# Filling two PSUM banks in turns, chunk by chunk, in a macaron layer (FFN, S4D convolution, FFN)

## The chip, the cores and the metric

One core of one Trainium2 chip runs the whole program. The metric is the device time of one execution in microseconds (us). Three runs of the kernel before gave 1369.08, 1369.99 and 1370.74 us; their median, 1369.99 us, is the time before. About 0.2% (2.7 us) is what a measurement of this kernel can tell from no change.

## What is computed

The input x has shape (4, 1024, 256), fp32. Three residual steps follow each other:

```
x = x + 0.5 * ffn(layernorm(x))
x = x + attn(layernorm(x))        # S4D: a causal convolution along the 1024 positions
x = x + 0.5 * ffn(layernorm(x))   # the same weights again

ffn:  h = silu(x @ w1.T * s1) * (x @ w2.T * s2)     # 256 -> 1024, two branches
      h = gelu(h @ h1.T * s3)                        # 1024 -> 1024
      h = gelu(h @ h2.T * s4)                        # 1024 -> 1024
      y = h @ w3.T * s5                              # 1024 -> 256
attn: y = irfft(rfft(x) * rfft(K))[:1024];  gelu(y) @ W.T + b
      K is computed from log_dt, A and C by exponentials, sines and cosines
```

The FFN weights hold only -1, 0 and 1; the scales s are separate vectors.

## The kernel before

**Blocks.** The 4096 tokens are cut into eight blocks of 512, "f0" to "f7" for the first FFN and "g0" to "g7" for the second. Activations lie transposed: 128 channels on the partitions, 512 tokens along the free side, so that 1024 channels are eight chunks of 128x512. f0 to f7, g0 and g1 are done one at a time by `ffn` (L374). The last six blocks are done as three pairs by `ffn_pair` (L416), whose two wide layers are Winograd products of quarters (L510) that the change leaves alone.

**Two parts.** An fp32 activation chunk is held as a rounded fp32r part and the rest: ScalarE (ACT) makes the first by a cast (L389, L401), VectorE (DVE) the second by a subtraction (`low_part`, L309). A weight tile is therefore multiplied twice, with the high part and with the low part. One output tile of a wide layer takes 8 chunks x 2 parts = 16 matmuls of 128x128 by 512 columns into one PSUM bank, one of the first layer 2 x 2 = 4, one of the last layer 16. `linear` (L362) issues them for one bank: all chunks in order, high then low.

**A block.** The first layer makes eight pairs of tiles `pa`, `pb` (eight chunks `ha`): Silu on ACT (L384), the product on DVE (L385), cast, low part. The second and third layer make eight tiles each (`p2` into chunks `h2`, `p3` into `h3`; the trace writes both as `p`): Gelu on ACT (L399), cast (L401), low part (L309). The last layer, `last_squares` (L603), makes two tiles `po` from the eight chunks `h3` with `w3` (L617), scales them on ACT (L628), transposes them on DVE (L629), adds the residual and stores. The last block of all ends in `last_tokens` (L636), which has the tokens on the partitions and is not changed.

So each layer needs all eight chunks of the layer before, and the last chunk comes out latest: Gelu, cast and subtraction still lie between the last matmul of one layer and the last inputs of the next.

**What else runs meanwhile.** After each tile of a wide layer `ffn` calls `ahead()` (the next block's norm and loading, `prepare` L1189) and `tick()` (L1245). A tick lets a generator called `aside` go on until it has spent an allowance of work (`STEP_WORK`, counted from DVE elements): first the convolution kernel (`kernel_steps` L833, with the exponentials of L820 and the sines and cosines of L740 and L741 on ACT, tile names `e_b`, `a_b`, `k_b`, `qd`, `p`, `po` on DVE, and products `pk` on TensorE at L883), later the convolution itself (`mix` L1036; transforms `pf`, `pi` and products `pw` on TensorE, `y` and `z` on DVE). When that pauses, weight sums and a check of the weights (`given`, `sign`) fill in. Work tiles come from a pool of 19 buffers ("half"), the chunks from one of 15 ("ring"), PSUM tiles from one of all 8 banks.

**The order.** The program is written in this order, but a scheduler then places the instructions of every engine, by its own estimate of when inputs and buffers are ready, and that order is fixed in the built program: each engine goes through its list in order, and waits where an input is late. The scheduler may already mix matmuls of two tiles where it expects a chunk late. Different functions on ACT (Gelu, Silu, square root, exponential, sine) need a table load where they alternate.

Of the kernel before, what the change touches and what calls it, by code (L numbers as in the profile page):

```python
# [18 lines left out]
P = 128  # L19
# [89 lines left out]
def macaron_layers(  # L109
# [24 lines left out]
    nc = tc.nc  # L134
    split = bad is not None
    wide = F32R if split else F32
    parts = 2 if split else 1
# [26 lines left out]
    def bank(name):  # L164
        return psum.tile([P, 512], F32, tag="ps", name=name)

    def half(name, *shape, dtype=F32):

        return work.tile([P, *(shape or (512,))], dtype, tag="half", name=name, bufs=19)

    def ring(name, *shape, dtype=F32):

        return work.tile([P, *shape], dtype, tag="ring", name=name, bufs=15)
# [7 lines left out]
    w1_sb = keep.tile([P, DC, HID], wide, name="w1_sb")  # L181
    w2_sb = keep.tile([P, DC, HID], wide, name="w2_sb")
# [124 lines left out]
    def low_part(t, src):  # L307

        return nc.vector.tensor_tensor(t[:, 1, :], src, t[:, 0, :].bitcast(F32), ALU.subtract)  # L309
# [49 lines left out]
            xt.append(t)  # L359
        return xt  # L360

    def linear(ps, w, m, acts):  # L362
        n = len(acts)
        for k in range(n):
            for part in range(parts):
                nc.tensor.matmul(  # L366
                    ps,
                    w[:, k, m * P : (m + 1) * P],
                    acts[k][:, part, :],
                    start=(k == 0 and part == 0),  # L370
                    stop=(k == n - 1 and part == parts - 1),
                )

    def ffn(xt, src, dst, blk, name, tick, ahead, final):  # L374


        ha = []
        for m in range(KH):
            pa, pb = bank(f"pa_{name}_{m}"), bank(f"pb_{name}_{m}")
            linear(pa, w1_sb, m, xt)  # L380
            linear(pb, w2_sb, m, xt)
            g = half(f"g_{name}_{m}")
            t = ring(f"ha_{name}_{m}", parts, TB, dtype=wide)
            nc.scalar.activation(g, pa, AF.Silu, scale=sc_sb[:, 0, m : m + 1])  # L384
            nc.vector.scalar_tensor_tensor(  # L385
                g if split else t[:, 0, :], pb, sc_sb[:, 1, m : m + 1], g, ALU.mult, ALU.mult
            )
            if split:
                nc.scalar.copy(t[:, 0, :], g)  # L389
                low_part(t, g)  # L390
            ha.append(t)
        for layer, w in ((2, h1_sb), (3, h2_sb)):
            hb = []
            for m in range(KH):
                ps = bank(f"p{layer}_{name}_{m}")
                linear(ps, w, m, ha)
                t = ring(f"h{layer}_{name}_{m}", parts, TB, dtype=wide)
                g = half(f"g{layer}_{name}_{m}") if split else t[:, 0, :]
                nc.scalar.activation(g, ps, AF.Gelu, scale=sc_sb[:, layer, m : m + 1])  # L399
                if split:  # L400
                    nc.scalar.copy(t[:, 0, :], g)  # L401
                    low_part(t, g)
                hb.append(t)
                ahead()
                if layer == 2 or m < KH - 1:
                    tick()
            ha = hb
        ahead(last=True)
        if name == "f0":
            nc.scalar.mul(w3s_half, w3s_half, 0.5)  # L410
        if final:
            last_tokens(ha, src, dst, blk, name)
        else:
            last_squares(ha, src, dst, blk, name)()

    def ffn_pair(xts, src, dst, blks, names, tick, ahead, final):  # L416

        pair_name = names[0]
        raw = raw_tiles(f"g_{pair_name}")
        for n, (xt, name) in enumerate(zip(xts, names)):  # L420
            for m in range(KH):
                pa, pb = bank(f"pa_{name}_{m}"), bank(f"pb_{name}_{m}")
                linear(pa, w1_sb, m, xt)
                linear(pb, w2_sb, m, xt)
                g = raw[m // QK, n][m % QK]
                nc.scalar.activation(g, pa, AF.Silu, scale=sc_sb[:, 0, m : m + 1])
                nc.vector.scalar_tensor_tensor(
                    g, pb, sc_sb[:, 1, m : m + 1], g, ALU.mult, ALU.mult
                )
            if n == 0:  # L430
                b11 = operand(raw[0, 0], f"b112_{pair_name}")
        calls = 0

        def step():
            nonlocal calls
            calls += 1
            if calls % 2 == 0:
                ahead()
                if calls < 2 * 7 * QK:
                    tick()  # L440

        raw, b11, _ = winograd(raw, b11, 2, pair_name, step)
        raw, c22, c12 = winograd(raw, b11, 3, pair_name, step)
        c11 = operand(raw[0, 0], f"hl00_{pair_name}")
        end_1 = last_squares(c12 + c22, src, dst, blks[1], names[1], QK)
        c21 = operand(raw[1, 0], f"hl10_{pair_name}")
        ahead(last=True)
        if final:
            end_1(nc.vector, nc.sync)
            last_tokens(c11 + c21, src, dst, blks[0], names[0])  # L450
        else:
            end_0 = last_squares(c11 + c21, src, dst, blks[0], names[0])
            end_1()
            end_0()


    def raw_tiles(name):


        return {  # L460
            (k, n): [
                late.tile([P, TB], F32, tag="raw", name=f"{name}_{k}{n}_{c}", bufs=4 * QK)
                for c in range(QK)
            ]
            for k, n in ((0, 0), (1, 1), (0, 1), (1, 0))
        }

    def operand(quarter, name):

        ops = []  # L470
        for c, src in enumerate(quarter):
            t = ring(f"{name}_{c}", parts, TB, dtype=wide)
            nc.scalar.copy(t[:, 0, :], src)
            low_part(t, src)
            ops.append(t)
        return ops
# [126 lines left out]
    def last_squares(acts, src, dst, blk, name, first=0):  # L603


        rest = []
        for k in range(DC):
            xr = half(f"xr_{name}_{k}", TB // SQ, SQ)
            for c in range(P // SQ):
                nc.sync.dma_start(xr[c * SQ : (c + 1) * SQ], in_squares(src, blk, k, c))  # L610
            rest.append(xr)
        banks = [bank(f"po_{name}_{k}") for k in range(DC)]
        order = [(first + k) % KH for k in range(KH)]
        for o, ps in enumerate(banks):
            for k in order:
                for part in range(parts):
                    nc.tensor.matmul(  # L617
                        ps,
                        w3_sb[:, k, o * P : (o + 1) * P],
                        acts[k][:, part, :],  # L620
                        start=(k == order[0] and part == 0),
                        stop=(k == order[-1] and part == parts - 1),
                    )

        def end(add_on=nc.gpsimd, queue=stores):
            for k, ps in enumerate(banks):
                o, y = half(f"o_{name}_{k}"), half(f"y_{name}_{k}", TB // SQ, SQ)
                nc.scalar.activation(o, ps, AF.Identity, scale=w3s_half[:, k : k + 1])  # L628
                nc.vector.transpose(y, o.rearrange("p (n s) -> p n s", s=SQ))  # L629
                add_on.tensor_tensor(y, rest[k], y, ALU.add)  # L630
                for c in range(P // SQ):
                    queue.dma_start(in_squares(dst, blk, k, c), y[c * SQ : (c + 1) * SQ])

        return end
# [610 lines left out]
    def tick():  # L1245


        nonlocal ticks, allowed, work_done
        ticks += 1
        allowed = min(allowed, work_done) + (  # L1250
            STEP_WORK_2 if ("f", n_blocks - 1) in done else STEP_WORK
        )
        while work_done < allowed:
            at = work_done
            if next(aside, PAUSE) is PAUSE:
                for _ in range(2):
                    if len(done) > 8 and allowed - work_done > OP_WORK + TB:
                        next(fillers, None)
                break
            if work_done == at:  # L1260
                work_done += MIN_WORK
# [7 lines left out]
    xt, last_split = transposed(x_first, "f0")  # L1269
    allowed = work_done  # L1270
    operands = [xt]
    for n, unit in enumerate(units):
# [6 lines left out]
        def ahead(last=False):  # L1279
            if last:  # L1280
                done.extend(("last layer", *b[::-1]) for b in upcoming)
            for step in steps:
                next(step, None)
# [102 lines left out]
```

## Time and profile before

| what | value |
|---|---|
| runs before | 1369.08, 1369.99, 1370.74 us |
| profiled execution, its own time | 1368.44 us |
| its span, first to last instruction | 1366.6 us |
| granted TensorE clock, mean | 0.998 |
| DVE busy | 1010.7 us (74%), 1889 instructions |
| ACT busy | 776.5 us (57%), 1236 instructions |
| POOL busy | 287.9 us (21%) |
| DMA moved | 159.99 MB, mean 117 GB/s |
| L366 matmuls, p_f from ha_f / from h_f | 1024 / 1024 instructions, 238.7 / 237.1 us |
| L617 matmuls, po_f | 256 instructions, 60.7 us |

A row of groups names line, engine, operation, output and inputs by the program's tile names without their numbers (p_f<-ha_f,h_sb is a tile of the second layer of some block of the first FFN), shape, count, busy time and mean duration. "PE" is the matmul side of TensorE, "PEld" its weight loads, "SP" the queue that issues most loads. In a timeline each row is a start, a length (both in us), the engine, the line and the instructions merged into it, and in brackets the idle time of the engine just before, with what ended it. The ends of matmuls are modelled: a pipelined matmul shows as some 390 ns though the next one starts sooner, so rows of matmuls overlap and starts are what counts.

### The profile page before, as it was taken

How to read it: one execution, taken by the hardware profiler on the slowest of the kernel's cores; microseconds unless marked ns; L12 is line 12 of the kernel's file. 1: busy time of each engine (PE TensorE's matmuls, PEld its weight loads, DVE VectorE, ACT ScalarE, POOL GpSimd, SP SyncE). 2: the span in 40 equal slices, each digit the busy share in tenths (PEclk: the TensorE clock that was granted, in tenths of full speed). 3: DMA queues.
4: the chain of work that ended last, by engine and by line, in shares of the span. 5: the costliest groups of instructions: out<-in, count | busy, mean ns of one | idle time of the engine just before them, and what ended most of it. 6: DMA issues, size and time to landing. Idle time of an engine off the chain costs nothing.

```text
span 1366.6 us, 18200 instructions
## 1 busy us (share of the span) xinstructions
PE 1351.7 (99%) x6300; PEld 1124.7 (82%) x6300; DVE 1010.7 (74%) x1889; ACT 776.5 (57%) x1236; POOL 287.9 (21%) x443
## 2 busy tenths in 40 slices
PE   8999999999999999999999999999999999999997
PEld 7888878888888888888888887888888888888886
DVE  6997885749965887668855799658885778568654
ACT  5985966454444543534545745436776576656663
POOL 4440220421205213420114012052300430040000
PEclk9999999999999999999999999999999999999999
DMA  9440121413125235354054352352655145521441
GB/s 357 109 142 5 31 62 39 143 36 123 40 93 199 64 108 190 122 183 123 23 168 116 112 154 47 116 168 79 212 160 168 31 141 179 173 64 62 162 131 49
DMA packets 125637, 159.99 MB, mean 117 GB/s; under 512 B 77968, under 2 KB 88208, under 8 KB 120160
## 3 DMA queue, kind: packets, MB, share of 16 engines
q1 hardware_dynamic: 103520, 99.94, 24.2%
q0 software_dynamic: 21744, 58.55, 13.6%
q8 instruction: 51, 0.84, 0.2%
q14 instruction: 50, 0.41, 0.1%
q10 hardware_dynamic: 272, 0.26, 0.1%
HBM read 120.95 MB, written 37.75 MB: 116 GB/s over the span
## 4 chain that ended last, share of the span: by engine, by line
PE 49%; DVE 4%; DMA 0%; issue 0%; ACT 0%; SPq 0%; DVEq 0%
PE p_g L366 7%; PE p2a_g L510 6%; PE p3a_g L510 6%; PE p3x_g L510 5%; PE p2x_g L510 5%; PE p_f L366 4%; PE pa_g L366 4%; PE pb_g L366 4%; PE po_g L617 3%; PE pi L1134 1%; PE pw L1159 1%; DVE y L155 1%; PE po_f L617 1%; PE pa_f L366 1%; PE pb_f L366 1%; PE pf_m L956 1%
## 5 line engine op out<-in xcount | busy, mean ns | idle before, releaser
L366 PE MATMUL p_f<-ha_f,h_sb 128*128 128x512 f32 x1024 | 238.7, 392 | 0.1
L366 PE MATMUL p_f<-h_f,h_sb 128*128 128x512 f32 x1024 | 237.1, 391 | 0.0
L366 PEld LDWEIGHTS p_f<-h_f,h_sb 128*128 128x128 f32 x1024 | 192.1, 188 | 39.7
L366 PEld LDWEIGHTS p_f<-ha_f,h_sb 128*128 128x128 f32 x1024 | 191.4, 188 | 40.4 <-DVE ha_f L309 0.8
L399 ACT ACTIVATE g_f<-p_f,sc_sb 128x512 f32<-128x512 f32 x128 | 87.4, 689 | 210.6 <-PE p_f L366 183.0
L309 DVE TENSOR_TENSOR h_f<-g_f,h_f 128x512 fp32r<-128x512 f32 x128 | 87.9, 689 | 112.8 <-ACT h_f L401 112.5
L401 ACT CAST h_f<-g_f 128x512 fp32r<-128x512 f32 x128 | 78.4, 619 | 3.1
L524 ACT ACTIVATE h_g<-h_g,sc_sb 128x512 f32<-128x512 f32 x72 | 52.0, 723 | 43.8 <-DVE h_g L480 43.6
L339 POOL DMA_DIRECT2D moved<-sq_f x56 | 30.6, 554 | 198.3 <-DVE sq_f L155 198.3
L366 PE MATMUL pa_f<-xt_f,w_sb 128*128 128x512 f32 x256 | 70.5, 391 | 1.3 <-DVE xt_f L321 0.7
L339 POOL DMA_DIRECT2D moved<-sq_g x64 | 34.9, 552 | 167.1 <-DVE sq_g L155 165.9
L366 PE MATMUL pb_f<-xt_f,w_sb 128*128 128x512 f32 x256 | 69.9, 389 | 0.0
L366 PE MATMUL pa_g<-xt_g,w_sb 128*128 128x512 f32 x256 | 68.9, 389 | 0.0
L366 PE MATMUL pb_g<-xt_g,w_sb 128*128 128x512 f32 x256 | 68.9, 389 | 0.0
L617 PE MATMUL po_f<-h_f,w_sb 128*128 128x512 f32 x256 | 60.7, 391 | 1.6 <-ACT h_f L401 0.9
L385 DVE SCALAR_TENSOR_TENSOR g_f<-pb_f,sc_sb,g_f 128x512 f32<-128x512 f32 x64 | 46.6, 745 | 20.2 <-ACT g_f L384 10.5
L366 PE MATMUL p_g<-ha_g,h_sb 128*128 128x512 f32 x256 | 59.4, 391 | 0.1
L366 PE MATMUL p_g<-h_g,h_sb 128*128 128x512 f32 x256 | 59.3, 391 | 0.0
L630 POOL TENSOR_TENSOR y_g<-xr_g,y_g 128x512 f32<-128x512 f32 x12 | 17.0, 1424 | 197.5 <-DVE y_g L629 183.8
L617 PEld LDWEIGHTS po_f<-h_f,w_sb 128*128 128x128 f32 x256 | 47.6, 188 | 13.0 <-DVE h_f L309 2.0
L366 PEld LDWEIGHTS pa_f<-xt_f,w_sb 128*128 128x128 f32 x256 | 48.0, 188 | 12.2 <-DVE xt_f L356 1.0
L399 ACT ACTIVATE g_g<-p_g,sc_sb 128x512 f32<-128x512 f32 x32 | 22.1, 689 | 60.8 <-PE p_g L366 49.5
(302 smaller groups left out, 2879.9 us busy)
## 6 DMA issues: line engine op xcount, KB each, us to landing
w<-q SPq DMA_DIRECT2D x42, 1024.0 KB, 5.0
q<-s POOLq DMA_DIRECT2D x40, 256.0 KB, 4.3
h_sb<-in_h_dram POOLq DMA_DIRECT2D x8, 1024.0 KB, 14.2
given<-in_h_dram SPq DMA_DIRECT2D x32, 256.0 KB, 3.4
kr<-k_hat SPq DMA_DIRECT2D x20, 256.0 KB, 2.7
ki<-k_hat SPq DMA_DIRECT2D x20, 256.0 KB, 3.0
q<-h_sb POOLq DMA_DIRECT2D x16, 256.0 KB, 4.4
xr_f<-in_x_dram SPq DMA_DIRECT2D x64, 64.0 KB, 2.5
```

The source lines that it names most:

```text
L155: return op(dst, *args, **kwargs)
L309: return nc.vector.tensor_tensor(t[:, 1, :], src, t[:, 0, :].bitcast(F32), ALU.subtract)
L339: stores.dma_start(moved[k].rearrange("(c r) a q -> a r c q", r=SQ)[a], sq[a * SQ : (a + 1) * SQ].rearrange("r c j s -> r c (j s)"),)
L366: nc.tensor.matmul(ps, w[:, k, m * P : (m + 1) * P], acts[k][:, part, :], start=(k == 0 and part == 0), stop=(k == n - 1 and part == parts ...
L385: nc.vector.scalar_tensor_tensor(g if split else t[:, 0, :], pb, sc_sb[:, 1, m : m + 1], g, ALU.mult, ALU.mult)
L399: nc.scalar.activation(g, ps, AF.Gelu, scale=sc_sb[:, layer, m : m + 1])
L401: nc.scalar.copy(t[:, 0, :], g)
L510: nc.tensor.matmul(ps, weights[:, c, m * P : (m + 1) * P], ops[c][:, part, :], start=(first and c == 0 and part == 0), stop=(c == QK - 1 a ...
L524: nc.scalar.activation(o, src, AF.Gelu, scale=sc_sb[:, layer, m : m + 1])
L617: nc.tensor.matmul(ps, w3_sb[:, k, o * P : (o + 1) * P], acts[k][:, part, :], start=(k == order[0] and part == 0), stop=(k == order[-1] an ...
L630: add_on.tensor_tensor(y, rest[k], y, ALU.add)
L956: nc.tensor.matmul(ps[e][:, part, :], m[:, e, part, :], rows_of(q + JQ * e), start=True, stop=True)
```

## The change

`linear` takes several (bank, weights, tile) at once and goes through the chunks on the outside, through the banks inside. Three callers use it with two banks: the two branches of the first layer (`pa` and `pb`, in `ffn` and `ffn_pair`), the first two tiles of each of the two wide layers in `ffn`, and, by its own loops, the last layer's two banks in `last_squares`. The number of matmuls, their operands and every other instruction that is written stay the same; only the order is written differently. In the wide layers both banks of the first two tiles are now taken before the first tile's Gelu, `ahead()` and `tick()`.

```diff
-    def linear(ps, w, m, acts):
+    def linear(outs, acts):
         n = len(acts)
         for k in range(n):
-            for part in range(parts):
-                nc.tensor.matmul(
-                    ps,
...
+            for ps, w, m in outs:
+                for part in range(parts):
+                    nc.tensor.matmul(
+                        ps,
+                        w[:, k, m * P : (m + 1) * P],
+                        acts[k][:, part, :],
+                        start=(k == 0 and part == 0),
+                        stop=(k == n - 1 and part == parts - 1),
+                    )
...
-            linear(pa, w1_sb, m, xt)
-            linear(pb, w2_sb, m, xt)
+            linear([(pa, w1_sb, m), (pb, w2_sb, m)], xt)
...
             hb = []
+            first = [bank(f"p{layer}_{name}_{m}") for m in range(2)]
+            linear([(ps, w, m) for m, ps in enumerate(first)], ha)
             for m in range(KH):
-                ps = bank(f"p{layer}_{name}_{m}")
-                linear(ps, w, m, ha)
+                if m < 2:
+                    ps = first[m]
+                else:
+                    ps = bank(f"p{layer}_{name}_{m}")
+                    linear([(ps, w, m)], ha)
...
-        for o, ps in enumerate(banks):
-            for k in order:
+        for k in order:
+            for o, ps in enumerate(banks):
                 for part in range(parts):
```

More of the change, by code (lines that the diff above doesn't have):

```diff
@@ L360, in parted @@
         return xt
-    def linear(ps, w, m, acts):
+    def linear(outs, acts):
         n = len(acts)
         for k in range(n):
-            for part in range(parts):
-                nc.tensor.matmul(
-                    ps,
[L368 to L372, printed above, removed]
+            for ps, w, m in outs:
[7 more added lines that the diff above has]
+                    )
     def ffn(xt, src, dst, blk, name, tick, ahead, final):
@@ L422, in ffn_pair @@
                 pa, pb = bank(f"pa_{name}_{m}"), bank(f"pb_{name}_{m}")
-                linear(pa, w1_sb, m, xt)
-                linear(pb, w2_sb, m, xt)
+                linear([(pa, w1_sb, m), (pb, w2_sb, m)], xt)
                 g = raw[m // QK, n][m % QK]
```

## The prediction

> **What bounds the kernel now.** I read the page's engine rows first, then who TensorE waits for, then the chain in order of time, then the stages with waits.
>
> ```profile
> span 1366.6 us, 18200 instructions
> PE 1351.7 (99%) x6300; PEld 1124.7 (82%) x6300; DVE 1010.7 (74%) x1889; ACT 776.5 (57%) x1236; POOL 287.9 (21%) x443
> ```
> ```profile
> PE po_f L617 <- ACT h_f L401: 0.9, 1, 0.9
> PE po_f L617 <- DVE h_f L309: 0.7, 1, 0.7
> PE po_g L617 <- DVE h_g L309: 0.6, 1, 0.6
> PE po_g L617 <- ACT h_g L401: 0.3, 1, 0.3
> ```
> ```profile
> 1096.98 7.25 PE p2a_g L510 x32
> ```
>
> TensorE (PE) is busy 99%, but its ends are modelled, so I go by starts: 32 wide matmuls in 7.25 us (third fence) is 227 ns each, and 5408 of them make 1226 us. All that PE waits for is listed in eight rows, 6.6 us together, of which 2.6 are the very first. Counting late starts instead of named waits, with the slow start after each pause, I find about 6 us in the body: 2.2 at f1's last layer (the po rows), 1.5 at g0's last layer, 0.9 at f6's, 0.4 at f0's, and 0.5 and 0.4 at the second layer of f1 and g1. The change can take away no more than these 6 us.
>
> Why so few: the scheduler already mixes banks where it expects a late chunk.
>
> ```profile
> 171.72 6.51 PE L617 MATMUL po_f<-h_f,w_sb 128*128 128x512 f32 x28
> 172.18 1.28 ACT L740 ACT_TABLE_LOAD   x1
> 173.47 0.63 ACT L740 ACTIVATE a_b<-a_b 128x512 f32<-128x512 f32 x1
> 174.01 0.71 ACT L741 ACTIVATE k_b<-k_b,cst_sb 128x512 f32<-128x512 f32 x1
> 176.43 1.28 ACT L399 ACT_TABLE_LOAD   x1 [1.71 <-DVE k_b L155]
> 177.73 0.69 ACT L399 ACTIVATE g_f<-p_f,sc_sb 128x512 f32<-128x512 f32 x1
> 178.44 0.62 ACT L401 CAST h_f<-g_f 128x512 fp32r<-128x512 f32 x1
> 179.12 0.73 PE L617 MATMUL po_f<-h_f,w_sb 128*128 128x512 f32 x2 [0.89 <-ACT h_f L401]
> 179.82 0.69 DVE L309 TENSOR_TENSOR h_f<-g_f,h_f 128x512 fp32r<-128x512 f32 x1
> 180.57 0.30 PEld L617 LDWEIGHTS po_f<-h_f,w_sb 128*128 128x128 f32 x2 [1.16 <-DVE h_f L309]
> ```
>
> At f1's last layer PE did 28 matmuls first: all seven ready chunks of *both* banks. The order that the change writes was in place, and PE still stood, because ACT put a sine/cosine with two table loads before the eighth tile's Gelu. What ends last here is the queue on ACT and DVE. The stages say the same:
>
> ```profile
> 36.00:90.00 54.00, 54.00 (x238) 44.24 (x237) 52.66 (x127) 49.87 (x68) 21.01 (x39) 1.00 0.46 140
> 792.00:830.00 38.00, 37.13 (x163) 29.95 (x162) 37.75 (x84) 16.09 (x23) 3.29 (x6) 1.00 0.47 131
> ```
> (start:end and length, then busy PE, PEld, DVE, ACT, POOL.) In f0's second half DVE is busy 52.7 of 54 us and ACT 49.9; in g0's last part DVE 37.75 of 38. There a chunk's time is set by what stands ahead of it on DVE and ACT.
>
> **The change part by part.** The built order of the changed kernel can be read without running it. Matmuls, DVE, POOL and DMA instructions are the same in number; ACT gets 7 more table loads. For each chunk I summed the DVE work ahead of its low part, by the durations in this trace, in both orders. They differ in two places only: f0, and g0's third and last layer. Elsewhere the last chunk stands as before, and its first use comes 14 matmuls later (28 instead of 14, +3.2 us).
>
> *First layer, pa and pb in turns.* The silu starts 2 matmuls (0.45 us) later for each pair of tiles; a pair takes 8 x 227 ns = 1.8 us, ACT needs 1.3 of it and DVE 1.35, and the chunk is needed 6.4 us later. Cost nothing; without the later first use of the chunk it would be 0.45 us a block.
>
> *Second and third layer, first two tiles in turns.* Takes away the 0.5 us at f1 and the 0.4 at g1: -0.9. Nothing else waits there, so the other 18 such boundaries give nothing. The two banks are taken 3.6 us earlier; eight tiles pa/pb held them and were read by then, so no bank wait.
>
> *pk blocks.* The longer head makes the scheduler cut five blocks of 16 pk products (f1 and f2) in two halves with 8 wide matmuls between.
>
> ```profile
> 111.64 0.61 PE L366 MATMUL p_f<-ha_f,h_sb 128*128 128x512 f32 x2
> 112.19 2.05 PE L883 MATMUL pk<-qd,p 128*64 128x32 f32 x32
> ```
> Around this block, single starts go 318 ns into it, and after it one of 335 instead of 227; with what lies between, a change to pk and back costs about 0.3 us. Five more: +1.5 (0.7 to 1.5, if only the change in counts).
>
> *Last layer, f0.* In the changed order DVE has the norm of block f3 and of f2, the products a_b, k_b and four qd ahead of f0's last low part: 7.1 us more than before, against a use that comes 3.2 us later. Why they moved: f0's first two tiles of layer two end together at 31.4 us, DVE idles some 2.5 us for them, and the kernel steps slide to later tiles. ACT: f0's third layer ends its first two tiles at 64.5 us instead of 60.5 (50 matmuls from 53.14 are ahead of that). From the first Gelu there to the last cast, before took 24.6 us (60.59 to 85.16), 0.7 of it waiting. The new list adds two table loads (2.6) and a sine and a cosine (1.3): 27.8 us, so the last high part is there at 92.3. PE starts this layer at 82.15 as before:
>
> ```profile
> 82.15 7.80 PE L617 MATMUL po_f<-h_f,w_sb 128*128 128x512 f32 x32
> ```
> and is done with 28 at 88.5. It then waits to 92.3, fills in with six matmuls of f1, and waits for the low part, by DVE at 94.3 to 96.6. Its 38 matmuls end at 94.7 to 97.1 instead of 90.8: a stall of 3.9 to 6.3, less the 0.4 of before. Value +4.7 (3.5 to 6): both queues are full, so a gain is excluded.
>
> [...]
>
> *Last layer, g0.* From 792.5 DVE has one idle gap of 0.25 us to 830. The changed order has the norm of g4 before the last two chunks: 3.4 us more ahead of the seventh low part, 3.1 ahead of the eighth. They come at 826.9 and 830.5; PE, from 819.29, needs the seventh at 825.2, then stands behind one g1 matmul that needs a copy which DVE makes at 829.5. It ends 35 matmuls at 831.1 instead of 827.2: 3.9 lost instead of 1.5. Value +2.4 (1 to 3.5).
>
> *Last layer, the others.* f1 and f6 have the same order on PE, ACT and DVE around the stall as before, and f1's begins with ACT work that PE itself released at 139 us: they stay, 0 (f6 could lose its 0.9). In the pairs the last layer has no gap: 0.
>
> *Banks in turns as such.* In the trace of before, a start after a change of bank comes 227.8 ns after the last (426 cases), without one 227.1. Some 750 more changes: +0.5, taken as +0.2. [...] Two tiles in turns end together, so nothing of the second covers the first's reading. [...] Only at the end of the program could it show: there the outputs' first half is read 3.6 us later, with DVE done at about 1354.4 and its next input there at 1354.7. Zero.
>
> **Sum**, on the profiled execution (1368.44 us, 1.8 over its span of 1366.6; the median of the runs is 1.55 higher): -0.9 + 1.5 + 4.7 + 2.4 + 0.2 = +7.9, from ends +4 to +12. I shade it to +7.5 for what f6 may give back: 1375.9 for a profiled execution, 1377.5 for the median.
>
> **The rivals.**
>
> *The shifts are swallowed, about no change* (18%): +1, 1371. If DVE or ACT reach f0's eighth chunk by 90.7 us, when PE needs it, f0 loses nothing; likewise g0 by 826.8. For it: the scheduler chose this order by its own estimate, with fillers only for six matmuls. Against: the busy rows above.
>
> *Faster* (7%): 1367. One mechanism: the moved norms and products stand in f0 and g0, where the late first use gives 3.2 us. If ACT's chain in f0 is shorter by over 4 us than my sum, the stalls of f0 and g0 (1.9) go as well as 0.9 in layer two and f6's 0.9, which pays for the pk changes at 0.7: -3.0. It decides at 88.5 us, the end of the 28 matmuls. Against it, ACT alone has 27.8 us of work from 64.5.
>
> *Banks in turns cost TensorE* (10%): 1386. At the program's start single matmuls in turns are 231 to 236 ns apart. If alternation does this, 2144 matmuls by 4 ns are +8.6 on top. Against: 227.8.
>
> **The numbers.** Forecast 65%: 1377.5, own range 1373 to 1382. Faster by over 0.2% (below 1367.2) 7%; within 0.2% 17%, mostly the second case; slower 76%. The range 1370.5 to 1384 takes in the swallowed case's upper part and both ends of the sum, and leaves out the faster case and most of the third.
>
> **What would show it.** Right: PE standing 4 to 6 us between 86 and 97 us and 3 to 4 between 823 and 831, waiting for ACT h_f and DVE h_f, h_g; f1's 2.2 us still there, later; no gap at layer two of f1 and g1; 13 blocks of pk; 227 ns between starts. Wrong: f0's last layer without a stall over 1 us, starts 231 ns apart, or waits of PE in the pairs or for banks.

## The result and the profile after

| kernel | median | runs | ratio to before (95%) |
|---|---|---|---|
| before, same chip | 1369.08 us | 5, 1367.78 to 1370.74 | |
| changed | 1377.52 us | 5, 1376.88 to 1377.67 | 1.0059 (1.0045 to 1.0074) |

The change costs 8.4 us. Its profiled execution took 1377.12 us and has a span of 1375.3 us, 8.7 more than before. First the page's head, then what TensorE (PE) waits for (engine, line, who was waited for: us in all, times, longest).

```profile
span 1375.3 us, 18182 instructions
...
PE 1355.8 (99%) x6300; PEld 1127.2 (82%) x6300; DVE 1012.8 (74%) x1889; ACT 781.3 (57%) x1243; POOL 287.9 (21%) x443
```
```profile
PE po_f L624 <- ACT h_f L408: 3.7, 3, 2.6
...
PE pa_g L369 <- DVE xt_g L356: 1.9, 1, 1.9
PE pa_f L369 <- DVE xt_f L356: 1.5, 1, 1.5
PE po_f L624 <- DVE h_f L309: 1.5, 2, 0.8
```

PE's share is 99% as before, and its busy time has even grown by 4.1 us: the page's first rows would not show where the time went. The waits do: po_f waited for ACT 0.9 us before and 3.7 now, and pa_g's 1.9 us is new. The timelines of those places show how they come about. PE in f0's last layer (start, length, instructions, and in brackets the idle time before and what ended it):

```profile
81.80 4.70 PE L624 MATMUL po_f<-h_f,w_sb 128*128 128x512 f32 x20
86.81 0.73 PE L624 MATMUL po_f<-h_f,w_sb 128*128 128x512 f32 x2 [0.31 <-ACT h_f L408]
88.33 1.65 PE L624 MATMUL po_f<-h_f,w_sb 128*128 128x512 f32 x6 [0.78 <-DVE h_f L309]
92.54 1.22 PE L624 MATMUL po_f<-h_f,w_sb 128*128 128x512 f32 x2 [2.57 <-ACT h_f L408]
93.56 0.63 PE L369 MATMUL pa_f<-xt_f,w_sb 128*128 128x512 f32 x1
...
95.83 0.63 PE L624 MATMUL po_f<-h_f,w_sb 128*128 128x512 f32 x2
```

PE did 28 matmuls by 90.0, stood for 2.57 us, put six matmuls of f1 in between, and did the last two at 95.83. Before, these 32 ran from 82.15 without a pause. What ACT and DVE did meanwhile, first in the changed kernel, then ACT before:

```profile
87.30 1.28 ACT L747 ACT_TABLE_LOAD   x1
88.59 0.63 ACT L747 ACTIVATE a_b<-a_b 128x512 f32<-128x512 f32 x1
89.13 0.71 ACT L748 ACTIVATE k_b<-k_b,cst_sb 128x512 f32<-128x512 f32 x1
...
89.85 1.28 ACT L406 ACT_TABLE_LOAD   x1
91.15 0.69 ACT L406 ACTIVATE g_f<-p_f,sc_sb 128x512 f32<-128x512 f32 x1
...
91.87 0.62 ACT L408 CAST h_f<-g_f 128x512 fp32r<-128x512 f32 x1
...
93.07 1.71 DVE L155 TENSOR_TENSOR qd<-k_b,a_b 64x256 f32<-64x256 f32 x4
94.81 0.69 DVE L309 TENSOR_TENSOR h_f<-g_f,h_f 128x512 fp32r<-128x512 f32 x1
```
```profile
84.56 0.60 ACT L401 CAST h_f<-g_f 128x512 fp32r<-128x512 f32 x1
...
86.48 0.63 ACT L740 ACTIVATE a_b<-a_b 128x512 f32<-128x512 f32 x1
```

A sine, a cosine and two table loads now stand ahead of the eighth Gelu; before, they came after its cast. On DVE four products `qd` stand ahead of its low part, which is there at 95.5. In g0's last layer PE waits for the seventh low part, and then behind a matmul of g1 whose copy DVE makes late, after the norm of another block (`x_g`). First g0 before, then changed:

```profile
826.16 0.73 PE L617 MATMUL po_g<-h_g,w_sb 128*128 128x512 f32 x2 [0.29 <-ACT h_g L401]
827.47 0.73 PE L617 MATMUL po_g<-h_g,w_sb 128*128 128x512 f32 x2 [0.58 <-DVE h_g L309]
```
```profile
833.84 0.73 PE L624 MATMUL po_g<-h_g,w_sb 128*128 128x512 f32 x2 [0.71 <-DVE h_g L309]
836.47 0.80 PE L369 MATMUL pa_g<-xt_g,w_sb 128*128 128x512 f32 x1 [1.90 <-DVE xt_g L356]
```
```profile
835.03 1.05 DVE L155 TENSOR_SCALAR x_g<-x_g,mv_g,rstd_g 128x256 f32<-128x256 f32 x3
836.00 0.75 DVE L356 CAST xt_g<-xf_g 128x512 fp32r<-128x512 f32 x2
```

The stages (start:end, length, busy PE, PEld, DVE, ACT, POOL, then PE's granted clock, DMA share, GB/s); g0's is taken 7 us later than before, since PE is 7 us later there:

```profile
36.00:90.00 54.00, 52.88 (x231) 42.83 (x229) 52.37 (x138) 51.31 (x68) 21.33 (x39) 1.00 0.46 140
799.00:837.00 38.00, 34.98 (x151) 28.09 (x150) 37.95 (x90) 20.06 (x27) 3.31 (x6) 0.99 0.42 128
...
82.00:100.00 18.00, 14.34 (x55) 10.71 (x54) 16.70 (x34) 14.06 (x18) 1.83 (x2) 0.91 0.19 29
```

DVE is as full as before in f0's second half, and ACT is fuller (51.3 of 54 instead of 49.9); in g0's last part DVE is full again (37.95 of 38). In the last row the granted clock is 0.91: after the pause, starts are 427 ns apart instead of 227, until 95.27. That is a cost which the prediction had not. f1's stall is where it was, 28 matmuls and then two waits (0.82 and 0.72 us; before 0.89 and 0.72):

```profile
177.38 6.51 PE L624 MATMUL po_f<-h_f,w_sb 128*128 128x512 f32 x28
184.72 0.73 PE L624 MATMUL po_f<-h_f,w_sb 128*128 128x512 f32 x2 [0.82 <-ACT h_f L408]
...
```

The pk blocks are cut as foreseen (13 instead of 8; three cuts in f1, two in f2), and 32 matmuls of a pair take as long as before:

```profile
116.80 1.12 PE L890 MATMUL pk<-qd,p 128*64 128x32 f32 x16
117.85 2.11 PE L369 MATMUL p_f<-ha_f,h_sb 128*128 128x512 f32 x8
...
```
```profile
1107.29 7.42 PE L516 MATMUL p2a_g<-b_g,w 128*128 128x512 f32 x32
```

(31 starts 227 ns apart and one length of 0.39 are 7.42.) To see where the time goes in all, I set the start of each matmul against the matmul at the same place in PE's list before. The difference is the lag, and a step is what the lag changes by over a stretch. The lag grows by 5.5 us over f0's last layer and f1's first tiles, 0.5 at f1's second layer, 0.7 at f2's, 0.9 at f6's last layer and 3.8 over g0's last and g1's first; it falls by 0.4 at the start and 0.4 at g1's second layer, and does not change in the pairs. At the last matmul it is 10.5 us. The end of the program takes 1.75 back.

### The profile page after: what moved, and what is told of

It reads as the page before. It is cut to its first block, busy times and chain, and to the rows that moved or that the text cites. A ratio compares the mean times of both kernels' runs of the same rounds, so it can differ in the third digit from the quotient of the medians.

```text
span 1375.3 us, 18182 instructions
## 1 busy us (share of the span) xinstructions
PE 1355.8 (99%) x6300; PEld 1127.2 (82%) x6300; DVE 1012.8 (74%) x1889; ACT 781.3 (57%) x1243; POOL 287.9 (21%) x443
## 4 chain that ended last, share of the span: by engine, by line
PE 85%; DVE 6%; ACT 4%; DMA 3%; issue 1%; POOL 0%; SPq 0%; DVEq 0%; ACTq 0%; POOLq 0%
PE p_f L369 26%; PE p_g L369 6%; PE p3a_g L516 6%; PE p2a_g L516 6%; PE p2x_g L516 5%; PE p3x_g L516 5%; PE pa_g L369 4%; PE pb_g L369 4%; PE pa_f L369 4%; PE pb_f L369 4%; PE po_g L624 3%; PE po_f L624 3%; PE pi L1141 2%; PE pf_m L963 2%; PE pw L1166 2%; DMA h_sb<-in_h_dram 2%
## 5 line engine op out<-in xcount | busy, mean ns | idle before, releaser
L369 PE MATMUL pa_f<-xt_f,w_sb 128*128 128x512 f32 x256 | 81.6, 393 | 2.2 <-DVE xt_f L356 1.5
L369 PE MATMUL pa_g<-xt_g,w_sb 128*128 128x512 f32 x256 | 79.8, 392 | 1.9 <-DVE xt_g L356 1.9
L369 PE MATMUL pb_f<-xt_f,w_sb 128*128 128x512 f32 x256 | 81.0, 391 | 0.0
L369 PE MATMUL pb_g<-xt_g,w_sb 128*128 128x512 f32 x256 | 79.2, 390 | 0.0
L406 ACT ACT_TABLE_LOAD x40 | 51.3, 1283 | 27.1 <-PE p_f L369 18.7
L369 PEld LDWEIGHTS pa_g<-xt_g,w_sb 128*128 128x128 f32 x256 | 48.4, 189 | 12.4 <-DVE xt_g L356 2.3
L309 DVE TENSOR_TENSOR ha_f<-g_f,ha_f 128x512 fp32r<-128x512 f32 x64 | 51.8, 832 | 8.6 <-ACT ha_f L391 8.0
```

The lines of the kernel that those rows point to most:

```text
L369: nc.tensor.matmul(ps, w[:, k, m * P : (m + 1) * P], acts[k][:, part, :], start=(k == 0 and part == 0), stop=(k == n - 1 and part == parts ...
```

## Experiments

**Theory A**: the wide layers' tiles in turns make the scheduler build another order in f0 and g0, in which side work stands ahead of the last chunks on ACT and DVE; PE waits for that. **Theory B**: the last layer in turns is the loss. **Theory C**: changes of bank cost PE some ns. The first three runs take the change apart by its three callers, the fourth by its blocks.

| run | what it is | median | before there | ratio (95%) |
|---|---|---|---|---|
| e1_last | last layer alone | 1367.29 | 1368.85 | 0.9992 (0.9985 to 0.9998) |
| e2_wide | wide layers alone | 1379.95 | 1368.85 | 1.0079 (1.0065 to 1.0093) |
| e3_first | first layer alone | 1368.86 | 1368.85 | 1.0000 (0.9992 to 1.0009) |
| e4_not_f0_g0 | all but f0's and g0's wide layers | 1368.43 | 1368.85 | 0.9997 (0.9989 to 1.0005) |
| e5_second_off | all but f0's, g0's second layer | 1372.29 | 1368.58 | 1.0029 (1.0018 to 1.0040) |
| e6_third_off | all but f0's, g0's third layer | 1374.36 | 1368.58 | 1.0040 (1.0027 to 1.0054) |
| e7_filled | changed, pauses filled | 1377.70 | 1368.58 | 1.0067 (1.0053 to 1.0080) |
| e8_end_alone | before, residual loads first | 1367.11 | 1368.58 | 0.9988 (0.9982 to 0.9995) |
| e9_dve_more | e1 with 21 additions more on DVE | 1372.64 | 1368.54 | 1.0031 (1.0020 to 1.0041) |
| e10_fewer_steps | e1 with less side work in f1, g0 | 1366.62 | 1368.54 | 0.9982 (0.9975 to 0.9989) |
| e11_fewer_steps_old | before with less side work | 1367.42 | 1368.54 | 0.9990 (0.9984 to 0.9997) |
| e12_end_and_steps | e8 and e11 together | 1365.44 | 1368.84 | 0.9976 (0.9967 to 0.9985) |

### Each caller alone

Only the last layer:

```diff
-            linear([(pa, w1_sb, m), (pb, w2_sb, m)], xt)
+            linear([(pa, w1_sb, m)], xt)
+            linear([(pb, w2_sb, m)], xt)
...
-            first = [bank(f"p{layer}_{name}_{m}") for m in range(2)]
+            turns = 2 if False else 0
+            first = [bank(f"p{layer}_{name}_{m}") for m in range(turns)]
...
-                if m < 2:
+                if m < turns:
```

> The change cut down to its last layer: the two output banks in turns, first and wide layers as before. The built order leaves ACT's and DVE's work in f0 and g0 as it was, pk in 8 blocks, 92 table loads; SP issues the two residual loads of g6 ahead of the stores of g7, as in the changed kernel. Theory A (the loss is made by the wide tiles in turns of f0 and g0, which move work on ACT and DVE ahead of the last chunks; the last layer in turns is innocent): no loss; f0's 0.4 us and a part of g0's 1.5 go, f1's 2.2 stay, the end of the program is 1.7 shorter: -1.5 to -3.5, so 1365.5 to 1367.5. Theory B (the last layer in turns makes the loss: both banks end late together, nothing is left to do under the last chunk): most of the +8.4, so 1374 to 1378. Theory C (a change of bank costs TensorE some ns): 480 of 2144 matmuls, 4 ns each, +2, less the 1.7 of the end: 1369.5.

Measured 1367.29. Theory B is out. f0's last layer is 0.4 us shorter, of which f1's first tiles give 0.3 back; g0's and f1's steps are 0.0: 28 matmuls under the last chunk instead of 14 gave almost nothing. At the last matmul PE is 0.2 us ahead; the rest of the 1.6 us gained lies behind it.

Only the wide layers (the first and the last layer as before):

```diff
-        for k in order:
-            for o, ps in enumerate(banks):
+        for o, ps in enumerate(banks):
+            for k in order:
```

> The change cut down to the first two tiles of the wide layers; first and last layer as before. The built order has 99 table loads and 13 pk blocks as in the changed kernel, the same 10 table loads in f0's third layer and the same 8 more DVE instructions there. Theory A: all of the loss and none of the gain at the end of the program: +9.5 to +12, so 1378.5 to 1381, with the same waits for h_f and h_g as in the changed kernel. Theory B: about no loss, 1368 to 1370.5. Theory C: 640 of 2144 matmuls, +2.6: 1371.5.

Measured 1379.95, +11.1: all of the loss. Its waits are those of the changed kernel to 0.1 us (po_f for ACT 3.6, pa_g for DVE 1.9).

Only the first layer (the wide and the last layers by the two edits above):

> The change cut down to the first layer: two branches in turns; wide and last layers as before. Same waits and the same order of SP as before. Theory A: nothing, 1369 +- 0.7 (the changed kernel's first layer of f0 starts 0.35 us sooner). Theory B: nothing. Theory C: 1024 of 2144 matmuls by 4 ns, +4: 1373.

Measured no difference. Theory C is out: 1024 of the matmuls in turns cost nothing. The starts say so too: with the banks taken from the built order, and starts over 280 ns left out, those of 128x512 in the changed kernel are 226.9 ns apart after a change of bank (1354 cases) and 226.8 without one (3950).

All of the change, but not the wide layers of f0 and g0:

```diff
+            turns = 2 if name not in ("f0", "g0") else 0
...
```

> The whole change but for the wide layers of f0 and g0, whose tiles come one after the other as before. The built order has 94 table loads, 13 pk blocks, and in f0's and g0's third layer the list of ACT and DVE as before. Theory A: the losses of f0 (5.5) and g0 (3.8) go, the pk cuts (+1.7), f6's 0.9 and the gain at the end (-1.7) stay: 1377.5 - 9.3 = 1368, 1366.5 to 1369.5. Theory B: as the changed kernel, 1376 to 1378. Theory C: 128 matmuls fewer in turns of 2144, so 1377.

Measured 1368.43: without two blocks of sixteen the change costs nothing that can be told. The lag shows what is hidden in this zero: +0.5 at f1's second layer, +0.7 at f2's, +1.1 at f6's last layer, -0.4 at g1's second, and -1.7 at the end.

### Which layer of f0 and g0

```diff
+            turns = 2 if not (layer == 2 and name in ("f0", "g0")) else 0
...
```

> The whole change, but in f0 and g0 the second layer's first two tiles come one after the other as before; their third layer stays in turns. In the built order f0's third layer has the list of ACT and DVE work of before (8 table loads, 43 other DVE instructions), g0's that of the changed kernel. Theory A1 (f0 loses because the second layer's two tiles end together and ACT's and DVE's other work slides behind the third layer's tiles): f0's 5.5 us go, g0's 3.8 stay, 1377.5 - 5.5 = 1372. Theory A2 (f0 loses because the third layer's own first two tiles end together at 64.5 us and ACT starts its chain of Gelus 4 us late): f0 keeps most of its loss, 1376 to 1377.5.

The same with layer 3:

> The whole change, but in f0 and g0 the third layer's first two tiles come one after the other as before; their second layer stays in turns. In the built order f0's third layer has the changed kernel's longer list (10 table loads, 51 other DVE instructions), g0's that of before. Theory A1: f0's 5.5 us stay, g0's 3.8 go, 1377.5 - 3.8 = 1373.7. Theory A2: f0's loss goes as well, since its chain of Gelus starts at 60.5 again: 1368 to 1369.

Measured 1372.29 and 1374.36, both near A1. The steps say it block by block: f0's is -0.1 in e5_second_off and 6.3 in e6_third_off, g0's 4.9 and 0.0 (in the changed kernel 5.5 and 3.8; in e5_second_off the granted clock around g0's pause, 820 to 845 us, is 0.86 instead of 0.93). So f0's loss belongs to its second layer, g0's to its third; why it is another layer in g0 no run shows. With A2 a cause falls: f0's third layer ends its first two tiles at 64 us not because they are in turns. With turns off they end at 64.0 and 64.4, with turns on (e5_second_off) at 59.9 and 60.2, and in the kernel before at 60.4 and 60.6: the scheduler had mixed these two tiles already. What moves them is the second layer, whose last cast ends at 56.7 us before and 56.3 in e5_second_off, but at 59.7 in the changed kernel and 60.0 in e6_third_off. It is late because of what the two tiles in turns do to DVE. From 28 to 45 us, before, changed and e5_second_off in this order (the third of the busy times is DVE's; e6_third_off has the changed kernel's 12.91):

```profile
28.00:45.00 17.00, 17.00 (x77) 14.08 (x76) 15.79 (x53) 12.63 (x19) 5.83 (x10) 1.00 1.01 245
```
```profile
28.00:45.00 17.00, 17.00 (x77) 14.08 (x76) 12.91 (x42) 11.47 (x17) 8.55 (x15) 1.00 1.11 276
```
```profile
28.00:45.00 17.00, 17.00 (x77) 14.08 (x76) 15.87 (x55) 12.63 (x20) 6.04 (x11) 1.00 1.08 242
```

Where the second layer is in turns, DVE is 2.9 us less busy, and one row of its timeline in the changed kernel has most of that:

```profile
32.58 0.69 DVE L309 TENSOR_TENSOR h_f<-g_f,h_f 128x512 fp32r<-128x512 f32 x1 [2.42 <-ACT h_f L408]
```

The first tile of f0's second layer ends at 30.6 us instead of 27.8, and DVE stands until its cast is there. PE runs on and pays more than 50 us later, when the kernel steps that slid back are in front of the last chunk. This way from DVE's idle time to the late chunk is read from the rows; no run changes that idle time alone.

### Does the slow clock after a pause cost anything

21 matmuls whose sums nobody reads fill PE's pauses:

```diff
+        extra = {"f0": 12, "g0": 9}.get(name, 0)
+        if extra:
+            idle = bank(f"idle_{name}")
         for k in order:
+            if extra and k == order[-1]:
+                for i in range(extra):
+                    nc.tensor.matmul(
+                        idle,
+                        w3_sb[:, order[-2], 0:P],
+                        acts[order[-2]][:, 0, :],
+                        start=(i == 0),
+                        stop=(i == extra - 1),
+                    )
```

> The changed kernel with 21 matmuls more on TensorE, whose sums nobody reads, in a bank of their own: 3 and 9 of 128x512 in the two longest pauses of f0's last layer, 2 and 7 in those of g0's. All other engines have the changed kernel's order. They take 21 x 227 ns = 4.8 us that TensorE else waits (gaps of 1.2 and 3.0 us in f0, 1.1 and 2.3 in g0). Theory H (after a pause of 2 to 3 us TensorE runs at half its clock for some 3 us, and the matmuls are 427 ns apart for that reason): the seven slow starts of each place come back to 227, -1.5 in each, so 1374.5. Theory N (the slow starts belong to those matmuls, to their operands or their banks): they stay, 1377.5. If the extra matmuls run into the end of a wait: up to +1.

Measured 1377.70: no gain, against theory H by the number. Yet the starts 427 ns apart are gone. PE in f0 of e7_filled:

```profile
90.48 2.22 PE L627 MATMUL idle_f<-h_f,w_sb 128*128 128x512 f32 x9
93.18 0.73 PE L636 MATMUL po_f<-h_f,w_sb 128*128 128x512 f32 x2 [0.48 <-ACT h_f L408]
93.84 0.50 PE L369 MATMUL pa_f<-xt_f,w_sb 128*128 128x512 f32 x1
...
96.20 0.73 PE L636 MATMUL po_f<-h_f,w_sb 128*128 128x512 f32 x2 [0.70 <-DVE h_f L309]
```

The six matmuls of f1 start 224 to 335 ns apart, but then PE stands 0.70 us for the low part, which DVE gives when it gives it. In f0 the slow clock had only filled the next wait, and f0's step in the lag is 5.5 with it and 5.6 without. In g0 nothing is waited for behind it: there the step is 2.4 in e7_filled and 3.8 in the changed kernel, so the slow clock costs 1.4. PE is 1.0 us ahead of the changed kernel at its last matmul (a late start of 0.6 taken in); in this execution the span ended 6.2 us after the last addition instead of 5.4. Whether the program as a whole gains 1 us by it, the two ratios, each known to some 2 us, can't say.

### The end of the program

```diff
...
+            rest = residual(src, blks[0], names[0])
             end_1(nc.vector, nc.sync)
-            last_tokens(c11 + c21, src, dst, blks[0], names[0])
+            last_tokens(c11 + c21, src, dst, blks[0], names[0], rest)
...
```

(`residual` holds the two loads that stood at the head of `last_tokens`.)

> The kernel before, with g6's two residual loads issued ahead of the eight stores of g7 on SP, as the changed kernel has it by its built order; all matmuls, ACT and POOL as before, and the last four DVE instructions in another order. Theory T (the end of the changed kernel is 1.75 us shorter because these loads no longer stand behind stores that wait for g7's sums): 1369 - 1.75 = 1367.2. Rival (it is shorter because the banks in turns bring the last outputs sooner): 1369.

Measured 1367.11, theory T. PE's lag at the last matmul is 0.3 us here and the span is 1.4 shorter, so the end itself is 1.7 shorter. The end of the kernel before (SPq are the instructions that SP issues), and then that of e8_end_alone:

```profile
1349.94 5.09 SPq L632 DMA_DIRECT2D out_dram<-y_g  x8
1355.14 1.16 SPq L641 DMA_DIRECT2D xr_g<-x  x2
...
1358.89 1.35 DVE L665 TENSOR_TENSOR y_g<-xr_g,y_g 128x512 f32<-128x512 f32 x3
1359.60 1.96 SPq L666 DMA_DIRECT2D out_dram<-y_g  x3
```
```profile
1350.23 5.12 SPq L633 DMA_DIRECT2D out_dram<-y_g  x8
...
1356.50 3.64 SPq L669 DMA_DIRECT2D out_dram<-y_g  x3
...
1359.35 0.42 DVE L668 TENSOR_TENSOR y_g<-xr_g,y_g 128x256 f32<-128x256 f32 x1
```

Before, two loads are queued behind eight stores that wait for g7's sums; all three additions wait for them and are done together at the very end. With the loads ahead, two of the three additions and their stores are over before the last sum is there.

### Work ahead on DVE alone

```diff
                     nc.scalar.copy(t[:, 0, :], g)
+                    if name == "f0" and layer == 3 and m == KH - 1:
+                        more = small.tile([P, TB // 2], F32, name="more", bufs=1)
+                        for i in range(21):
+                            nc.vector.tensor_tensor(
+                                more,
+                                hb[-1][:, 1, : TB // 2].bitcast(F32),
+                                g[:, : TB // 2] if i == 0 else more,
+                                ALU.add,
+                            )
                     low_part(t, g)
```

> The change cut down to its last layer (as the first run, 1367.3), with 21 additions of 128x256 more on DVE in f0, which write a tile that nobody reads, between the eighth tile's cast and its low part: some 7.1 us at about 0.34 each, the DVE work that the changed kernel has ahead of that low part. ACT's list in f0 stays as before, with 8 table loads. Theory A1 (DVE's list alone makes f0's stall): the low part comes at 94 to 96 instead of 87, TensorE stands some 5 to 6 us and starts slowly behind it: +5 to +7, 1372.5 to 1374.5. Rival (the two table loads and the sine and cosine on ACT make it, DVE's part is absorbed): +0 to +2, up to 1369.5.

Measured 1372.64, the number that A1 gives, but by another place. The scheduler put the eighth low part ahead of nearly all of the additions (at 86.56, as without them), and PE waits elsewhere, for f1's inputs:

```profile
PE pa_f L369 <- DVE xt_f L309: 3.0, 1, 3.0
```

So the experiment doesn't tell how much of f0's wait is DVE's and how much ACT's. It shows that DVE's list alone costs PE 5.7 us of lag with ACT's 8 table loads unchanged, of which three more cuts of pk blocks are 1.0. For f0 itself the changed kernel's trace tells one half: DVE has no idle time there from 79.5 to 98 us, so the low part at 95.5 is late by DVE's own list, and PE would have stood for it even if ACT's cast had come sooner.

### Less side work ahead of the last chunks

On top of e1_last:

```diff
-                if layer == 2 or m < KH - 1:
+                if layer == 2 or m < KH - {"f1": 3, "g0": 2}.get(name, 1):
                     tick()
```

> The change cut down to its last layer, and in the third layer f1 asks for no side work after its sixth and seventh tile and g0 for none after its seventh; that work comes with later tiles. In f1 DVE has 27 other instructions instead of 36 and ACT 8 table loads instead of 9, in g0 DVE 57 instead of 60. Theory A (a chunk's time is set by what stands ahead of it on ACT and DVE): f1's 2.2 us, g0's 1.5 and a part of f6's 0.9 go: 1367.3 - 3.7 = 1363.6, from 1363 to 1365. Rival (the side work comes back later and makes a stall there, or the kernel's tail of side work ends later): 1366 to 1368.

The same edit alone:

> The kernel before with the same side work left out in f1's and g0's third layer, and nothing of the change. If the last layer in turns matters to the gain (28 matmuls under the last chunk instead of 14): f1 and g0 keep 1 us or more of their stalls, 1367 to 1368.5. If only the lists on ACT and DVE matter: they go here as well, 1369 - 3.7 = 1365.3, and 1.7 less if the end of the program has g6's residual loads first, which it has not in the built order.

Measured 1366.62 and 1367.42. The first is the rival's number and, by the steps, for the rival's reason; the second falls in the range in which the last layer in turns was to matter, and the steps speak against that. f1's last layer gains 2.2 us in both and g0's 1.5 and 1.4: the stalls of f1 and g0 go when the lists are shorter, and the order of the two banks doesn't matter, since in e11_fewer_steps_old the scheduler mixes them anyway. f6's 0.9 and the 0.5 at f1's second layer go too. But most of it is given back where the work comes later. What PE waits for in e10_fewer_steps:

```profile
PE pa_f L369 <- DVE xt_f L356: 1.6, 1, 1.6
PE p_f L369 <- DVE h_f L309: 1.4, 1, 1.4
```

Both are new: the first at 361.6 us, where f4's first layer begins (the lag grows by 2.3 us there in both runs), the second at 513.6 in f5's third layer (2.1 us, in e11_fewer_steps_old 0.8). At g1's end 1.1 and 1.0 more come.

> The kernel before with two edits and nothing of the change: g6's residual loads ahead of g7's stores (measured alone: 1367.1), and the side work of the run before left out in f1's and g0's third layer (measured alone: 1367.4). If the two are independent (one at the end of the program, one at f1, f5, f6 and g0): 1368.5 - 1.4 - 1.1 = 1366.0, 1365 to 1366.8. If the side work's gain is given back at the end: 1367.

The two edits together give 1365.44, 3.4 below before, where their sum is 2.6: no more apart than the intervals allow, and nothing given back. This is the fastest version tried, and it has nothing of the change.

## Why the prediction was right

The sign came out, and the size nearly (+7.5 forecast, +8.4 measured), because the main step was right: the built orders of f0 and g0 differ, and PE waits for it. That the totals agree to 0.02 us (1377.5 and 1377.52) is luck: the kernel before took 1369.08 us beside the changed one, 0.9 less than the 1369.99 from which the forecast started. The terms, by PE's lag:

| step | forecast | measured |
|---|---|---|
| second layer of f1 and g1 | -0.9 | -0.9 (f1 -0.5, which with three cuts makes +0.5; g1 -0.4) |
| five pk blocks cut | +1.5 | +1.7 (0.34 each) |
| f0's last layer | +4.7 | +5.5 |
| g0's last layer | +2.4 | +3.8, of which 1.4 slow clock |
| f1's and f6's stalls | 0, perhaps -0.9 | f1 -0.1, f6 +0.9 |
| changes of bank | +0.2 | 0 |
| end of the program | 0 | -1.75 |
| not forecast: start, rest of f | | -0.5 |

*f0.* The last high part was forecast for 92.3 and came at 92.5, the last low part for 94.3 to 96.6 and came at 95.5. The low part is in the middle of its range, and so was the value taken; the 0.8 more are the 0.35 us by which the changed run was ahead until then, and 0.33 from the low part's end to PE's next start. The two table loads were counted at 2.6: each took 1.28, and the Gelu behind the second started 1.30 after it (89.85, 91.15). The step counted 50 matmuls ahead of the third layer's first two tiles without saying whose turns put them there; e6_third_off shows that it is the second layer's alone.

*g0.* The wait itself is 2.4, as summed, and e7_filled shows it bare. What failed is that the matmuls behind a wait were counted at 227 ns.

*f6.* The step said that f6 could only lose its 0.9; it gained as much: PE waits 1.52 us instead of 0.60 for the same copy of f7's input. Two things add up. Where the wide tiles are in turns, DVE comes 0.5 us later to a norm (`x_g`) ahead of f6's last layer; in e5_second_off, which has that alone, PE waits 1.10. Where DVE loses it I have not settled. The other part is no work of the change: e8_end_alone has the orders of before in f6, and PE waits 1.05 there (e3_first 1.11, e9_dve_more 1.04; e1_last 0.60). One load of the check of the weights came later, ACT's `sign` waits for it, and behind that DVE's sum and the copy. Before, e8_end_alone, changed:

```profile
634.26 0.63 ACT L704 ACTIVATE sign<-given 128x512 f32<-128x512 f32 x1 [0.91 <-DMA given<-in_h_dram]
```
```profile
635.18 0.63 ACT L707 ACTIVATE sign<-given 128x512 f32<-128x512 f32 x1 [1.91 <-DMA given<-in_h_dram]
```
```profile
641.85 0.63 ACT L711 ACTIVATE sign<-given 128x512 f32<-128x512 f32 x1 [1.90 <-DMA given<-in_h_dram]
```

From issue to landing the load took 3.6 us before, 4.2 in e8_end_alone and 4.3 in the changed kernel. The same list is not the same time, and not even the same in two kernels that have it. The shading from +7.9 to +7.5 went the wrong way.

*The end.* It was costed at zero by looking at PE and DVE alone. The loads of g6 on SP moved past eight stores, and that queue was not looked at. They move with the last layer in turns (e1_last has it, e2_wide not), and e8_end_alone shows the 1.7 with that one edit.

*The start.* Its -0.35 is no work of the change either: e7_filled starts 0.2 late.

So the change's +8.4 is as close to +7.5 as it is because +0.8, +1.4 and +0.9 that were missed stand against -1.75 and -0.5. The sum's upper end is +10.6 by its own terms, not +12. Of the rivals, the costly change of bank has no case (e3_first). The swallowed shifts failed where the prediction said they would, at 90.7 us: the eighth low part came 4.8 us after that. The faster case needed ACT's chain over 4 us shorter; it was 0.2 longer.

## What to carry to other kernels

Where a scheduler fixes the order, what a rewritten loop does is to be read from every engine's built list, the store queue's too; here the order of matmuls itself was worth 0.9 us, since the scheduler already mixed banks, and two blocks of sixteen made all of the loss. When two tiles end together, the engines behind them can first starve and then be late: in f0's second layer DVE stood 2.4 us, and TensorE paid 5.5 us more than 50 us later. And look for the cheap thing at the end: two loads ahead of eight stores gave 1.5 us, more than the order of the matmuls did.

## What the hardware did that I had not expected

After a pause, PE's starts can be 427 ns apart, with a first one of 593. In the changed kernel this follows pauses of 2.57 and 1.90 us and lasts about 3 us; the granted clock is 0.50 from 92.6 to 95.2 us and from 836.5 to 839.0. In e5_second_off it follows g0's pause of 1.9 us. In e6_third_off the starts behind f0's pause of 2.55 us, from 92.81 on, are at first 0.22 to 0.34 us apart, and the slow ones (0.41 to 0.43) begin at 94.52, 1.7 us behind it, and go on to 97.70. The granted clock from 820 to 845 us in the changed kernel, in e5_second_off, then in e7_filled with the pauses filled:

```profile
820.00:845.00 25.00, 21.98 (x88) 17.08 (x87) 21.70 (x48) 13.18 (x19) 3.74 (x5) 0.93 0.36 90
```
```profile
820.00:845.00 25.00, 21.98 (x83) 16.98 (x82) 19.56 (x37) 13.55 (x20) 7.78 (x10) 0.86 0.33 70
```
```profile
820.00:845.00 25.00, 24.04 (x103) 18.91 (x102) 23.12 (x50) 14.89 (x21) 4.59 (x6) 1.00 0.39 95
```

It doesn't follow from the length of one pause: the 3.02 us in e9_dve_more, with no other pause around, were followed by a start after 0.33 us and then by starts of 230 ns at a clock of 1.00, while in f0 and g0 of the changed kernel two shorter waits of 0.3 to 0.8 us came in the 6 us before the long one. Whether those short waits decide it, or something else, no run shows.
